# Attention scores from split queries and keys stacked to K = 128, heads taken group by group, and image 0's convolution inputs made in other steps

## The chip, the cores and the metric

The kernel runs on one core of one Trainium2 chip. The metric is the device time of one execution in microseconds (us), the median of the runs shown. Engines are named as in the profile: PE (TensorE matmuls), PEld (its weight loads), DVE (VectorE), ACT (ScalarE), POOL (GpSimd), SP (SyncE, which here issues DMAs).

## The reference

x has four images of 256 channels and 48 x 48 pixels (N = 2304 tokens). Two layers follow each other, both with a residual. Cut to what matters:

```python
def layer0(v):                                   # v = group_norm(x)
    h = relu(bn(conv3x3(v)))                     # 256 -> 256
    q, k, v = split(qkv_w @ h + qkv_b)           # 8 heads of d = 32
    attn = softmax(q.T @ k * d**-0.5)            # 2304 x 2304 per head
    return proj_w @ (v @ attn.T) + proj_b
def layer1(v):                                   # v = group_norm(x)
    g = conv3x3(v)                               # 45 logits per pixel
    outs = [v]
    for i, d in enumerate((1, 6, 12, 24, 36)):
        w = softmax(g[:, 9*i:9*i+9])             # over 9 taps
        outs.append(sum(shift(v, tap_k, d) * w[k] for k in range(9)))
    return batch_norm(conv1x1(concat(outs)))     # over all four images
x = x + layer0(group_norm(x))
x = x + layer1(group_norm(x))
```

## The kernel before

All arithmetic is fp32, but for one f32r matmul in the filters. Channels lie on the 128 partitions in two halves (NH = 2, index g); each half holds four heads of 32 channels. The program is written out in full, image after image, and each engine runs its instructions strictly in that written order; so do the DMAs that SP issues. Tiles come from pools with a fixed number of buffers, and an instruction that needs a buffer waits until its last user is done. DMAs of one queue take eight semaphores in turn, so a DMA also waits for the landing of the one eight before it.

Image 0 first runs its convolution and its q, k and v products alone. Then, for each image b, come two stages: attention of image b, and the dynamic filters of image b. Into the filter stage of image b the convolution and the q, k, v products of image b + 1 are woven, paced by how much DVE work a filter tap has. The last image's filter stage stands alone (`alone`), and after it the batch norm is applied and the output stored.

**Convolution** (`conv`, `inputs`, `outputs`, class `Made`). The 3 x 3 convolution is done in a transformed domain along rows: six positions, taken in the order `ORDER = (1, 2, 3, 4, 0, 5)`, each with its own transformed weights u and transformed input rows `v[i]`, for two halves of the rows. The input rows are made in three steps (`inputs(stage, g)`), by ACT's multiplications and, in image 0, DVE's additions; a table `when` says before which position each step is written. In image 0 the weights are made as well (`Made.pair`, `Made.__call__`), and stored to DRAM for the other images (`taken` reads them back). The results pass through a ring of two PSUM banks (`psum_tile` from `psc`); ACT copies positions 1 and 3 to tiles of tag `m1` (four buffers), DVE combines the others.

**q, k and v** (`conv_qkv`). For each of six chunks of 384 tokens, each half g and each of q and k, PE makes one product (two 128-row matmuls), ACT adds the bias and writes it to an SBUF tile that holds the whole image, and DVE takes the largest absolute value of it for a safety bound. Then the v products follow.

**Attention** (`attention`). A unit is 512 queries of one half g; 2304 is four times 512 and 256 over, so each image has eight units, two per stretch of 512 queries (both halves), and a ninth that holds the last 256 queries of both halves side by side. Each unit has 18 steps, one for every 128 keys. A step m has these parts, and the step's `weigh` is written after the next step's `scores`:

- `scores` (L891): for each of the four heads a matmul with K = 32, on the head's own 32 partitions, to two PSUM tiles of two banks each (three such tiles exist); then two ACT exps (L900) of 128 x 1024 to `p` (three buffers).
- `weigh` (L921): four matmuls with M = 32 that add v times p to `num`; and either DVE adds p to `acc` (L938), or, in steps 5 and 11, PE adds its column sums to `den` (L947).
- At the unit's end ACT copies `num` out (L943). Two steps into the next unit, `close` adds the column sums of `acc` to `den`, and DVE transposes, inverts and multiplies (L956 to L964).

Every fp32 matmul is two instructions in the trace, two passes. While units run, `project` (L996, L1005) makes the output projection of finished chunks, and twelve ACT instructions (L1528) normalise the next image. Before attention, SP is given the reloads of the image rows (`load_pad`, L1507) and the first weights of the next convolution.

**Dynamic filters** (`dynamic_filters`). For each tap PE spreads one row of filter weights over the partitions (L1239, an f32r matmul in one pass), DVE multiplies it with the shifted image (L1256, L1263), POOL adds it up (L1276), and PE mixes the result into the output (L1185). `pump` decides from `rate` how many of the waiting PE parts (mixes, the next logits, the next image's convolution) are written after each tap. Finished chunks are stored by SP (L1207).

Of the kernel before, what the change touches and what calls it, by code (L numbers as in the profile page):

```python
# [8 lines left out]
F32 = mybir.dt.float32  # L9
# [8 lines left out]
P = 128  # L18
# [27 lines left out]
def conv_preact_kernel(  # L46
# [479 lines left out]

    with tc.tile_pool(name="w", bufs=1) as wpool, tc.tile_pool(
# [21 lines left out]
        zeros = wpool.tile([P, D], F32, tag="zeros", name="zeros")  # L549
        nc.gpsimd.memset(zeros, 0.0)  # L550

        pick = wpool.tile([P, NG], F32R, tag="pick", name="pick")


        e1 = wpool.tile([P, 2 * TPC, 2, 64], F32, tag="e1", name="e1")
        nc.gpsimd.memset(e1, 0.0)
# [8 lines left out]

        lg = wpool.tile([P, CH], F32, tag="lg", name="lg")
        nc.gpsimd.memset(lg, 0.0)
# [25 lines left out]
        class Norm:  # L593


            def __init__(self, tag, b):
                self.name = f"{tag}_{b}"
                self.st = small.tile([P, NH, NCK, 6], F32, tag=f"st{tag}", name=f"st{self.name}")
                self.mv = small.tile([P, NH, 2], F32, tag=f"mv{tag}", name=f"mv{self.name}")
# [56 lines left out]
        class Made:  # L656
# [23 lines left out]
            def __call__(self, i):  # L680
                w, u = self.w, self.u
                if i == 3:
                    self.pair(3, range(NH), self.other)
# [11 lines left out]
        def conv(b, gn, psum_tile, weights, ready, pool, hid):  # L695
# [55 lines left out]
            def outputs(i, g, o, m):  # L751
# [15 lines left out]
                if i in (1, 3):  # L767
                    first[at] = pool.tile([P, TN], F32, tag="m1", name=f"m_{b}_{i}_{at}", bufs=4)
# [17 lines left out]
            if b == 0:  # L786
                when = {(0, 0): [(0, 0), (0, 1)], (1, 0): [(1, 0), (1, 1)], (3, 0): [(2, 0), (2, 1)]}
            else:
                when = {
                    (0, 0): [(0, 0), (0, 1), (1, 0), (1, 1)], (0, 1): [(2, 0), (2, 1)]  # L790
                }
            ahead = ready
            for at, i in enumerate(ORDER):
                u = ahead
                for g in range(2):
                    for stage, gg in when.get((at, g), ()):
                        inputs(stage, gg)
# [19 lines left out]
        def conv_qkv(b, gn, psum_tile, weights, ready, pool):  # L817

            hid = keep("h", f"hid_{b}")
            yield from conv(b, gn, psum_tile, weights, ready, pool, hid)  # L820
            q, k_ = keep("q", f"q_{b}"), keep("k", f"k_{b}")
            vT = act.tile([P, NT, C], F32, tag="v", name=f"vT_{b}")
            qkv[b] = q, k_, vT

            part = small.tile([P, 2, NH, NCK], F32, tag="qkpart", name=f"qkpart_{b}")
            top = small.tile([P, 2, NH], F32, tag="qktop", name=f"qktop_{b}")
            for c in range(NCK):
                cols = slice(c * CH, (c + 1) * CH)
                for g in range(NH):
                    for s, dst, bias in ((0, q, Q_B), (1, k_, K_B)):  # L830
                        pq = psum_tile(f"pq_{b}_{c}_{g}_{s}")
                        for i in range(NH):
# [6 lines left out]
                            )  # L839
                        nc.scalar.activation(  # L840
                            dst[:, g, cols], pq[:, :CH], AF.Identity, bias=vec[:, bias, g : g + 1]
                        )
                        nc.vector.tensor_reduce(
                            part[:, s, g, c : c + 1], dst[:, g, cols], AX.X, ALU.max,
                            apply_absolute_value=True,
                        )
                        yield 2 * MM
            for t in range(0, NT, 2):
# [23 lines left out]
        def attention(b, q, k_, vT, pools, spare, project):  # L872
# [3 lines left out]
            ao = keep("h", f"ao_{b}")  # L876

            whole, rest = N // QC * QC, N % QC
            units = [[(g, q0, QC, 0)] for q0 in range(0, whole, QC) for g in range(NH)]
            units.append([(g, whole, rest, g * rest) for g in range(NH)])  # L880
            assert NH * rest == QC
            heads = [slice(j * D, (j + 1) * D) for j in range(4)]

# [3 lines left out]
            def scores(u, m):  # L887
                ss = [ps2(f"se_{b}_{u}_{m}_{pair}") for pair in range(2)]
                for g, q0, n, at in units[u]:
                    for j, r in enumerate(heads):  # L890
                        nc.tensor.matmul(  # L891
                            ss[j // 2][:, j % 2, at : at + n],
                            k_[r, g, m * P : (m + 1) * P],
                            q[r, g, q0 : q0 + n],
                            start=True,
                            stop=True,
                        )
                p = work0.tile([P, 4, QC], F32, tag="p", name=f"p_{b}_{u}_{m}", bufs=3)
# [8 lines left out]
            def weigh(u, m, p):  # L907
                if m == 0:
# [5 lines left out]
                several = len(units[u]) > 1  # L914
                if several and m == 0:

                    for j, r in enumerate(heads):
                        nc.tensor.matmul(st["num"][r, :], zeros, p[:, j, :], start=True, stop=False)
                for i, (g, q0, n, at) in enumerate(units[u]):
                    for j, r in enumerate(heads):  # L920
                        nc.tensor.matmul(  # L921
                            st["num"][r, at : at + n],
                            vT[:, m, g * P + j * D : g * P + (j + 1) * D],
                            p[:, j, at : at + n],
                            start=(m == 0 and not several),
                            stop=(m == NT - 1 and i == len(units[u]) - 1),
                        )
                end = u == len(units) - 1
                direct = (DIRECT[0], NT - 1) if end else DIRECT
                if m in direct:  # L930
                    if m == DIRECT[0]:
                        st["den"] = ps_a.tile([P, 512], F32, tag="den", name=f"den_{b}_{u}")
                    sums(u, p, m == DIRECT[0], False)
                elif m == 0:
                    st["first"] = p
                else:
                    other = st["first"] if m == 1 else st["acc"]
                    nc.vector.tensor_tensor(st["acc"], other, p, ALU.add)  # L938
                if end:
                    st["out"] = st["num"]  # L940
                elif m == NT - 1:
                    st["out"] = work0.tile([P, QC], F32, tag="out", name=f"no_{b}_{u}")
                    nc.scalar.copy(st["out"], st["num"])  # L943

            def sums(u, rhs, start, stop):
                for j, r in enumerate(heads):
                    nc.tensor.matmul(  # L947
                        state[u]["den"][r, :], ones, rhs[:, j, :], start=start, stop=stop
                    )

            def close(u):

                sums(u, state[u]["acc"], False, True)
                st = state.pop(u)
                t = work0.tile([P, QC], F32, tag="rden", name=f"rt_{b}_{u}", bufs=1)
                nc.vector.transpose(t, st["den"])  # L956
                rc = work0.tile([P, QC // D], F32, tag="rc", name=f"rc_{b}_{u}")
                nc.vector.reciprocal(rc, t.rearrange("p (k d) -> p k d", d=D)[:, :, 0])
                nc.vector.transpose(
                    t.rearrange("p (k d) -> p k d", d=D),  # L960
                    rc.unsqueeze(2).to_broadcast([P, QC // D, D]),
                )
                for g, q0, n, at in units[u]:
                    nc.vector.tensor_tensor(  # L964
                        ao[:, g, q0 : q0 + n], st["out"][:, at : at + n], t[:, at : at + n],
                        ALU.mult,
                    )

            steps = [(u, m) for u in range(len(units)) for m in range(NT)]
            prev = None  # L970
            chunk = 0
            for i, (u, m) in enumerate(steps):
                ps = scores(u, m)
                if prev is not None:
                    weigh(*steps[i - 1], prev)
                prev = ps
                if m == 2 and u:
                    close(u - 1)
                if m == 6 and u % NH == 0:
                    while (chunk + 1) * CH <= units[u][0][1]:  # L980
                        project(chunk, ao, ps2(f"pp_{b}_{chunk}"))
                        chunk += 1
                if m > 2 and u > 1 and spare:
# [50 lines left out]
        def dynamic_filters(b, ao, chunk, norm, other, pools):  # L1034
# [89 lines left out]
            alone = b == B - 1  # L1124
# [494 lines left out]
```

## Time and profile before

| what | value |
|---|---|
| median of 3 runs | 3092.05 us (3091.05 to 3093.03) |
| profiled execution, its own time | 3093.91 us |
| its span | 3092.1 us |
| PE busy | 2875.9 us (93%) |
| DVE busy | 2354.6 us (76%) |
| ACT busy | 1547.9 us (50%) |
| POOL busy | 1108.2 us (36%) |
| scores and exps, image 0 | 155.4 to 548.3 us |
| scores and exps, image 1 | 889.8 to 1286.2 us |
| scores and exps, image 2 | 1627.9 to 2024.4 us |
| scores and exps, image 3 | 2364.0 to 2756.4 us |
| filter taps (L1263), image 0 | 593.7 to 880.6 us |
| filter taps (L1263), image 3 | 2800.6 to 3048.6 us |

Busy time is the time in which an engine had at least one instruction running, and matmul ends are modelled, so PE's share says less than the starts of its instructions. In a group's row, "x" is the number of instructions, then come busy time and the mean of one in ns, then the engine's idle time before them and what ended it.

### The profile page before, as it was taken

How to read it: one execution, taken by the hardware profiler on the slowest of the kernel's cores; microseconds unless marked ns; L12 is line 12 of the kernel's file. 1: busy time of each engine (PE TensorE's matmuls, PEld its weight loads, DVE VectorE, ACT ScalarE, POOL GpSimd, SP SyncE). 2: the span in 40 equal slices, each digit the busy share in tenths (PEclk: the TensorE clock that was granted, in tenths of full speed). 3: DMA queues.
4: the chain of work that ended last, by engine and by line, in shares of the span. 5: the costliest groups of instructions: out<-in, count | busy, mean ns of one | idle time of the engine just before them, and what ended most of it. 6: DMA issues, size and time to landing. Idle time of an engine off the chain costs nothing. (4 is left out here: it accounts for less than half of the span.)

```text
span 3092.1 us, 43492 instructions
## 1 busy us (share of the span) xinstructions
PE 2875.9 (93%) x17782; PEld 1326.9 (43%) x17782; DVE 2354.6 (76%) x2280; ACT 1547.9 (50%) x1812; POOL 1108.2 (36%) x833
## 2 busy tenths in 40 slices
PE   6999999998999999998999999999899999988984
PEld 4722224465542222465662222356565222244663
DVE  5478888578768888767867888867776898876766
ACT  3388878201248887600217887830114888750003
POOL 0000000797940000388890000069794000006794
PEclk9999999999999999999999999999999999998997
DMA  4400000001040000010003000000001000022004
GB/s 160 104 1 6 6 11 7 26 32 35 16 82 6 1 6 11 22 35 31 29 6 77 6 6 11 6 27 26 21 6 42 6 1 6 11 73 102 1 1 174
DMA packets 77968, 95.57 MB, mean 31 GB/s; under 512 B 52144, under 2 KB 66752, under 8 KB 75968
## 3 DMA queue, kind: packets, MB, share of 16 engines
q1 hardware_dynamic: 76960, 87.31, 9.8%
q0 software_dynamic: 800, 5.41, 0.4%
q8 instruction: 141, 2.31, 0.3%
q14 instruction: 67, 0.55, 0.1%
HBM read 62.03 MB, written 30.67 MB: 30 GB/s over the span
## 5 line engine op out<-in xcount | busy, mean ns | idle before, releaser
L900 ACT ACTIVATE p<-se 128x1024 f32<-128x1024 f32 x1296 | 1258.4, 1025 | 281.3 <-PE se L891 235.8
L938 DVE TENSOR_TENSOR acc<-acc,p 128x2048 f32<-128x2048 f32 x504 | 1154.6, 2291 | 110.1 <-ACT p L900 71.0
L1276 POOL TENSOR_TENSOR cat<-cat,prod 128x752 f32<-128x752 f32 (+7 forms) x734 | 992.4, 1361 | 589.3 <-issue 442.9
L891 PE MATMUL se<-q,k 32*128 32x512 f32 (+1 forms) x5760 | 806.9, 593 | 10.5 <-ACT p L900 7.4
L1263 DVE TENSOR_TENSOR prod<-wb,pad 128x768 f32<-128x768 f32 (+7 forms) x768 | 550.7, 746 | 208.9 <-PE wb L1239 171.7
L921 PE MATMUL num<-p,vT 128*32 128x512 f32 (+1 forms) x5760 | 695.3, 562 | 9.6 <-ACT no L943 7.4
L891 PEld LDWEIGHTS se<-q,k 32*128 32x128 f32 x5760 | 294.3, 183 | 525.6 <-issue 422.5
L716 POOL TENSOR_TENSOR cv_q<-pad,cv_q 128x600 f32<-128x600 f32 x3 | 5.4, 1791 | 1350.0 <-ACT cv_q L714 1350.0
L1239 PE MATMUL wb<-w,pick 128*128 128x384 f32 (+3 forms) x888 | 425.2, 517 | 24.1 <-DVE prod L1263 22.3
L1185 PE MATMUL py<-cat,wsc 128*128 128x384 f32 x960 | 364.8, 508 | 33.4 <-POOL cat L1276 33.2
L921 PEld LDWEIGHTS num<-p,vT 128*32 128x32 f32 x5760 | 121.8, 108 | 488.5 <-issue 439.5
L1185 PEld LDWEIGHTS py<-cat,wsc 128*128 128x128 f32 x960 | 183.1, 197 | 135.2 <-POOL cat L1276 42.7
L1239 PEld LDWEIGHTS wb<-w,pick 128*128 128x128 f32 x888 | 166.9, 193 | 140.1 <-DVE prod L1263 45.5
L805 PE MATMUL pc<-cv_q,u 128*128 128x288 f32 x576 | 168.8, 425 | 7.1 <-DVE cv_q L718 7.1
L805 PE MATMUL pc<-cv_k,u 128*128 128x288 f32 x576 | 163.2, 414 | 9.3 <-DVE cs L772 6.5
L1061 PE MATMUL pg<-pad,wcat 128*45 128x384 f32 x864 | 153.3, 498 | 2.4 <-DVE pad L589 1.5
L1256 DVE TENSOR_TENSOR cat<-wb,pad 128x768 f32<-128x768 f32 x120 | 114.2, 952 | 46.4 <-PE wb L1239 46.1
L744 ACT ACTIVATE hid<-yt,bn_t_f,bn_s 128x288 f32<-128x288 f32 x64 | 39.4, 625 | 202.6 <-DVE yt L757 116.2
L833 PE MATMUL pq<-hid,wqkv 128*128 128x384 f32 x384 | 135.7, 486 | 0.0
L938 DVE TENSOR_TENSOR acc<-p,p 128x2048 f32<-128x2048 f32 x36 | 82.5, 2292 | 65.1 <-ACT p L900 65.1
L805 PEld LDWEIGHTS pc<-cv_q,u 128*128 128x128 f32 x576 | 111.5, 200 | 35.1 <-DVE cv_q L718 7.2
L805 PEld LDWEIGHTS pc<-cv_k,u 128*128 128x128 f32 x576 | 108.2, 193 | 37.4 <-DVE cs L772 6.9
(209 smaller groups left out, 1676.7 us busy)
## 6 DMA issues: line engine op xcount, KB each, us to landing
pad<-in_x SPq DMA_DIRECT2D x14, 1152.0 KB, 15.2
u<-u_d SPq DMA_DIRECT2D x18, 768.0 KB, 4.3
x_d<-pad SPq DMA_DIRECT2D x48, 192.0 KB, 2.5
xst<-in_x SPq DMA_DIRECT2D x36, 192.0 KB, 2.4
y_d<-y SPq DMA_DIRECT2D x18, 384.0 KB, 2.7
u_d<-u SPq DMA_DIRECT2D x6, 768.0 KB, 3.7
y<-y_d SPq DMA_DIRECT2D x2, 2304.0 KB, 14.0
x<-x_d SPq DMA_DIRECT2D x2, 2304.0 KB, 21.3
```

Source lines behind the costliest of these rows:

```text
L805: nc.tensor.matmul(m, u[:, h, kx, o * P : (o + 1) * P], halves[g][:, h, i, :, kx : kx + WW], start=(h == 0 and kx == 0), stop=(h == NH - 1 ...
L833: nc.tensor.matmul(pq[:, :CH], wqkv[:, i, s, g * P : (g + 1) * P], hid[:, i, cols], start=(i == 0), stop=(i == NH - 1),)
L891: nc.tensor.matmul(ss[j // 2][:, j % 2, at : at + n], k_[r, g, m * P : (m + 1) * P], q[r, g, q0 : q0 + n], start=True, stop=True,)
L900: nc.scalar.activation(p[:, 2 * pair : 2 * pair + 2, :], ss[pair], AF.Exp, scale=QS)
L921: nc.tensor.matmul(st["num"][r, at : at + n], vT[:, m, g * P + j * D : g * P + (j + 1) * D], p[:, j, at : at + n], start=(m == 0 and not s ...
L938: nc.vector.tensor_tensor(st["acc"], other, p, ALU.add)
L1061: nc.tensor.matmul(pg[64 * s : 64 * s + NG, :CH], wcat[:, i, k, :], window(gn, i, (c + s) * R, k // 3 - 1, k % 3 - 1), start=(i == 0 and k ...
L1185: nc.tensor.matmul(to, wsc[:, n * NH + i, o * P : (o + 1) * P], rhs(i), start=(n == 0 and i == 0), stop=(last and i == NH - 1),)
L1239: nc.tensor.matmul(pw[:, : nr * WW], pick[:, k : k + 1].to_broadcast([P, P]), w[:, l0 * WW : l1 * WW], start=True, stop=True,)
L1256: nc.vector.tensor_tensor(catv, wb, src, ALU.mult)
L1263: nc.vector.tensor_tensor(pv, wb, src, ALU.mult)
L1276: nc.gpsimd.tensor_tensor(dst, dst, pv, ALU.add)
```

## The change

It has three parts.

1. **Scores.** `conv_qkv` no longer keeps q and k whole in SBUF. ACT writes the biased product rounded to f32r (`head`), DVE writes what the rounding left (`tail`, a scalar_tensor_tensor that reads PSUM and `head`), and SP stores both to DRAM (`qk_d`). `stack` reads them back so that one head's operands fill 128 partitions: head, tail, head, tail of the keys, and head, head, tail, tail of the queries. A score block is then one f32r matmul with K = 128 per head. Keys of one half g lie in two tiles, reloaded for g = 1 as the last unit of g = 0 uses them up; queries are loaded a unit ahead by 16 DMAs per unit.
2. **Units.** They now run half by half: four units of 512 and one of 256 queries for g = 0, then for g = 1. A unit of 256 takes two blocks of keys per step, so nine steps. `close`'s and `num`'s work tiles are parts of one buffer of the pool of transformed weights; the row reloads and the next weights are issued after the first two units' queries (`begin`). The `zeros` matmuls go; `lg` and `e1` are made once per image.
3. **Image 0's convolution.** The second half of the rows is normalised after the first input step of the first half; the second input step of both halves and the weights for positions 3 and 4 are made before the second half of position 1; the third step comes one half position earlier. In the last filter stage `rate` loses its factor of 1.5.

```diff
+    qk_d = tc.dram_tile([2, 2, P, NH, N], F32, name="qk_d")
...
-                if i == 3:
-                    self.pair(3, range(NH), self.other)
...
             if b == 0:
-                when = {(0, 0): [(0, 0), (0, 1)], (1, 0): [(1, 0), (1, 1)], (3, 0): [(2, 0), (2, 1)]}
+                when = {
+                    (0, 0): [(0, 0), 0, (0, 1)], (0, 1): [(1, 0), (1, 1), 1],
+                    (2, 1): [(2, 0), (2, 1)],
+                }
...
+        def stack(dst, s, parts, g, j0, nj, cols):
+            for at, part in enumerate(parts):
+                nc.sync.dma_start(
+                    out=dst[at * D : (at + 1) * D].bitcast(F32),
+                    in_=qk_d[s, part, j0 * D : (j0 + nj) * D, g, cols].rearrange(
+                        "(j d) n -> d j n", d=D
+                    ),
+                )
+        def keys_of(keys, g, c):
+            cols = slice(c * CH, (c + 1) * CH)
+            for pair in range(2):
+                stack(keys[pair][:, :, cols], 1, (0, 1, 0, 1), g, 2 * pair, 2, cols)
...
-                        nc.scalar.activation(
-                            dst[:, g, cols], pq[:, :CH], AF.Identity, bias=vec[:, bias, g : g + 1]
+                        head, tail = (
+                            pool.tile([P, CH], F32, tag="m1", name=f"{n}_{b}_{c}_{g}_{s}", bufs=4)
+                            for n in ("head", "tail")
+                        )
+                        of = vec[:, bias, g : g + 1]
+                        nc.scalar.activation(
+                            head.bitcast(F32R), pq[:, :CH], AF.Identity, bias=of
+                        )
+                        nc.vector.scalar_tensor_tensor(
+                            out=tail.bitcast(F32R), in0=pq[:, :CH], scalar=of, in1=head,
+                            op0=ALU.add, op1=ALU.subtract,
                         )
...
+                        nc.sync.dma_start(out=qk_d[s, 0, :, g, cols], in_=head)
+                        nc.sync.dma_start(out=qk_d[s, 1, :, g, cols], in_=tail)
                         yield 2 * MM
+                if c:
+                    keys_of(keys, 0, c - 1)
+            keys_of(keys, 0, NCK - 1)
...
+            units = [(g, q0, min(QC, N - q0)) for g in range(NH) for q0 in range(0, N, QC)]
...
+            def queries(u, js):
+                g, q0, n = units[u]
+                for j in js:
+                    t = work0.tile([P, 1, QC], F32R, tag="qs", name=f"qs_{b}_{u}_{j}", bufs=8)
+                    stack(t[:, :, :n], 0, (0, 0, 1, 1), g, j, 1, slice(q0, q0 + n))
+                    qs[u, j] = t
...
-                for g, q0, n, at in units[u]:
-                    for j, r in enumerate(heads):
+                n = units[u][2]
+                for j in range(4):
+                    for m, cols in blocks(u, i):
                         nc.tensor.matmul(
-                            ss[j // 2][:, j % 2, at : at + n],
-                            k_[r, g, m * P : (m + 1) * P],
-                            q[r, g, q0 : q0 + n],
+                            ss[j // 2][:, j % 2, cols],
+                            keys[j // 2][:, j % 2, m * P : (m + 1) * P],
+                            qs[u, j][:, 0, :n],
                             start=True,
                             stop=True,
                         )
...
+            for u in range(2):
+                queries(u, range(4))
+            begin()
...
+                if i == 0 and 0 < u < len(units) - 1:
+                    queries(u + 1, range(4))
...
+                if u + 1 < len(units) and units[u + 1][0] != g:
+                    while (fetched + 1) * CH <= (blocks(u, i)[-1][0] + 1) * P:
+                        keys_of(keys, units[u + 1][0], fetched)
+                        fetched += 1
...
-            if alone:
-                mixes *= 1.5
...
+                        rows(0, HH // 2 + 2)
+                        weights.pair(ORDER[0], [1], weights.home)
+                        between = (
+                            lambda: rows(HH // 2 + 2, HH),
+                            lambda: weights.pair(3, range(NH), weights.other),
+                        )
```

## The prediction

> **What bounds the kernel now.** First the page's costliest groups, those of attention's scores.
>
> ```profile
> L900 ACT ACTIVATE p<-se 128x1024 f32<-128x1024 f32 x1296 | 1258.4, 1025 | 281.3 <-PE se L891 235.8
> ...
> L891 PE MATMUL se<-q,k 32*128 32x512 f32 (+1 forms) x5760 | 806.9, 593 | 10.5 <-ACT p L900 7.4
> ```
>
> The exp waits for the scores (235.8 us), the scores hardly for anything. Next the table of stretches: attention of image 0, the q and k products of image 0, and those of image 1, which lie inside the filter stage.
>
> ```profile
> 156.00:548.00 392.00, 388.33 (x3122) 118.36 (x3114) 335.86 (x191) 326.22 (x350) 0.00 (x0) 1.00 0.03 6
> 107.00:138.00 31.00, 31.00 (x98) 18.28 (x97) 15.49 (x29) 13.97 (x24) 0.00 (x0) 1.00 0.61 120
> 776.00:850.00 74.00, 69.52 (x241) 43.43 (x239) 57.41 (x92) 15.42 (x26) 69.64 (x54) 1.00 0.06 17
> ```
>
> Columns: length, then busy PE, PEld, DVE, ACT, POOL. PE leads in all three; DVE has 56 us free per image's attention, but 17 of 74 in the last row. Third, PE's timeline in attention:
>
> ```profile
> 982.94 1.14 PE L891 MATMUL se<-q,k 32*128 32x512 f32 x8
> 984.01 1.06 PE L921 MATMUL num<-p,vT 128*32 128x512 f32 x8
> 985.01 1.31 PE L891 MATMUL se<-q,k 32*128 32x512 f32 x8
> 986.25 1.06 PE L921 MATMUL num<-p,vT 128*32 128x512 f32 x8
> ...
> 994.06 2.85 PE L996 MATMUL pp<-ao,wp 128*128 128x384 f32 x8
> 996.84 1.14 PE L891 MATMUL se<-q,k 32*128 32x512 f32 x8
> ```
>
> Starts count here, since ends are modelled. A score block takes 1.07 us unhindered (982.94 to 984.01) and 1.24 when its second pair must wait for exp to free a PSUM pair; num takes 1.00. A plain step averages 2.155 (exp starts 2.13 and 2.18 apart), and a plain unit is 41.55 (L943, one copy per unit: 936.83, 978.37): 18 x 2.155 plus two direct sums of 0.88 and a closing one of 0.97. So PE's sum alone sets a unit.
>
> **Scores.** Before, four heads run at once in 32-row tiles, each in two fp32 passes. L996 shows the parts: 2.78 us for eight passes of 384 columns. Passes of L1185 start 0.322 apart, so 8 x 0.322 = 2.58 and 0.20 is left for the first weight load and the change of tiling. A 512-column pass is 0.427 and 2 x 0.427 + 0.20 = 1.05: the 1.07 is explained. The new matmul is f32r, one pass, K = 128, four in a row. Its price is in the q and k products, where a filter matmul (f32r, 384 columns) stands between fp32 passes:
>
> ```profile
> 843.10 1.45 PE L833 MATMUL pq<-hid,wqkv 128*128 128x384 f32 x4
> 844.10 0.63 PE L1239 MATMUL wb<-w,pick 128*128 128x384 f32 x1
> 844.57 1.45 PE L833 MATMUL pq<-hid,wqkv 128*128 128x384 f32 x4
> ```
>
> 1.47 - 4 x 0.322 = 0.18; start to start in the instruction records the least is 0.169. An fp32 column costs 0.84 ns, so half of that is 0.160 for 384: 0.009 is added per instruction. For 512 columns: 0.213 + 0.009 = 0.222. A new block is 0.20 + 4 x 0.222 = **1.09**; from below 0.20 + 4 x 0.213 = 1.05, from above 4 x 0.24 (0.18 scaled) + 0.20 = 1.16. One pass for four heads in a row is thus worth what two passes of four heads at once are worth; the gain is only that pairs now finish 0.45 us apart, so that the wait for exp (0.09 on average) goes. The step becomes 2.085, 0.07 less.
>
> The Trainium skill speaks against even that: "TensorE: Matmul & The Clock Gate", The mechanism, says that a weight load overlaps running matmuls only when the row group differs, and here all four use all rows. By it each block would show three more loads. The rows disagree: L1185's loads start 2 ns after the matmul before, and the next matmul starts 0.322 on, pure column time. The same page (Back-to-back issue gap) gives N / 2.4 + 2.5 ns, 216 ns for 512 columns: a block of 1.06, which would add 0.03 us to the gain per step.
>
> Per image: eight full units, 8 x 18 x 0.07 = -10.1. The shared last unit (41.72) becomes two half units of nine steps: each block is 8 matmuls of 256 columns (0.107 + 0.009, say 0.119; most of 192 columns took 0.110) + 0.20 = 1.15, so 18 x 2.15 + five sums 4.6 = 43.3, +1.6. In the 12 steps that also hold L1528's normalisation ACT is the bound (two exps issued 0.92 apart and 0.7, over 2.085) and nothing is gained: +0.8 in three images. Sum **-32 us** (-60 with 1.05, +8 with 1.16). DVE's add (2.396 start to start) is longer than a step and lags 0.31 per step; three p buffers leave some 1.8, and direct steps give 2 back, so I take no stall.
>
> **Start of attention.** Rows of the timeline at image 1:
>
> ```profile
> 889.74 0.51 SPq L1207 DMA_DIRECT2D y_d<-y  x1
> ...
> 889.76 1.99 PE L891 MATMUL se<-q,k 32*128 32x512 f32 x12 [0.93 <-ACT y L1203]
> ...
> 893.07 3.77 ACT L900 ACTIVATE p<-se 128x1024 f32<-128x1024 f32 x4 [3.36 <-DMA y_d<-y]
> ```
>
> Scores are ready today and exp starts when y's store lands. In the new order on SP the 16 loads of unit 0's queries stand behind that store, and the first waits for its landing too. SP issues 0.37 apart (72.32 to 72.69) to 0.50 (x_first: four in 2.02); I take 0.42, and 2.2 to land (1.9 and 2.4 for 192 KB). Head 3 is there at 893.1 + 6.7 + 2.2 = 902.0, its exp at 902.4 against 894.0: +8.4. After an idle PE the next 24 passes of the convolution took 8.23 for 5.98 (rows below); I add 1. Three images: **+28** (20 to 35). For image 0 the v products (15.7 us) cover the loads: +1. The pads' four loads (6 us each on SP) and u_1 move behind 32 query loads; they are needed some 100 us later (L1528 at 996), so free; unit 2's queries behind them still precede unit 2.
>
> **Split of q and k.** Each of 24 products per image gains a scalar_tensor_tensor on DVE (0.61 by L1005) and two stores, on four m1 buffers: two products in flight. A buffer pair turns in exp-like head 0.58 + DVE 0.61 + issue 0.42 + landing 2.4 + hand-overs 0.2 = 4.2 us, 2.1 per product, against 1.30 on PE (31.1 / 24). Each chunk of four also puts eight key loads (3.4 us) on SP ahead of the next stores, of which about 1.3 is not hidden: 9.7 per chunk. Image 0: 8.4 + 5 x 9.7 = 57 for 31, less 4 that the v products overlap: **+22** (from 93 issues x 0.37 = 34: +4, to +30). Images 1 to 3 spread the products 3.1 us apart, so the buffers turn in time, but DVE gains 14.7 us in the 74 us row with 17 free. PE and POOL lead there (94%), so I take a third: **+14** (0 to 44). If that cover is gone, it is the 44.
>
> **Image 0's convolution.**
>
> ```profile
> 48.20 8.23 PE L805 MATMUL pc<-cv_k,u 128*128 128x288 f32 x24 [6.49 <-DVE cs L772]
> ...
> 67.90 5.98 PE L805 MATMUL pc<-cv_q,u 128*128 128x288 f32 x24
> 76.10 4.14 PE L805 MATMUL pc<-cv_k,u 128*128 128x288 f32 x9 [2.22 <-DVE cs L775]
> ```
>
> The second-stage inputs and the pair for u_3 now run while the first products do, so DVE is free when the outputs come: 6.49 falls to 0.5, the slow passes (8.23 - 5.98) go, 2.22 goes, and half the rows' normalisation (0.82) leaves the start: **-11** (-12 to -8). In the last filter stage the factor 1.5 goes, and mixes lie one tap further apart: -2 (-6 to 4). Memsets of lg and e1 fall on an idle POOL; zeros goes: 0.
>
> Sum: -32 + 28 + 1 + 22 + 14 - 11 - 2 = **+20**. The profiled execution took 3093.91 (span 3092.1) and becomes 3114; the median, 3092.05, becomes **3112 us**.
>
> **Rivals.** *Free switch, faster:* between whole-array matmuls and the column tiles the first load and the drain (0.20) are hidden, so a block is 0.90. A unit would be 36.2, but DVE's 15 adds and closing (38.5) then bound it at 39.0: -2.6 x 9 = -92 in four images, 3052. For it: L996 to L891 shows 0.20 only at fp32. Against it: f32r matmuls are followed by L1061's column tiles 0.262 to 0.268 later, by L805's 0.171. It decides from a gain of 13 us per image on, a step under 2.065. *Exposed loads, slower:* each of four loads (0.107, as for transposes 0.108 apart) is seen: block 1.41, step 2.40, +0.25 x 162 x 4 = +162, 3294 with the other terms. L1185's rows are against it. *The split fills the filter stage:* DVE's 14.7 is paid whole and late stores hold DVE and ACT: +44 for +14, 3142. For it: 94% on PE and POOL at once.
>
> **Chances.** Forecast 0.62 (3075 to 3140); free switch 0.20; exposed loads 0.06; full filter stage 0.12. About 0.2%, 6 us, is what a measurement can tell from no change: between 3086 and 3098 I put 0.10 (0.09 of the forecast's, 0.01 of the free switch's), faster 0.25 (0.06 and 0.19), slower 0.65. The range 3060 to 3150 reaches into the free switch below and past the full stage above.
>
> **What would show it.** Right: score blocks of 1.05 to 1.16, plain units near 40.3, first exps some 8 us after y lands, q and k products of image 0 over some 55 us with head waiting for DMA, no 6.49 gap. Wrong: blocks under 1.0 or over 1.3; head 3's queries landed before y; products still 31 us long.

## The result, and the profile after

The changed kernel took 3119.03 us (median of 4 runs, 3116.03 to 3121.70) beside 3091.55 us of the kernel before on the same chip: a ratio of 1.0091, 95% interval 1.0074 to 1.0109, some 28 us slower. The forecast was 3112. The profiled execution took 3118.67 us, its span 3116.9, which is 24.8 more than the span before.

First the costliest groups of the page, the two lines that answer to those of before:

```profile
L958 ACT ACTIVATE p<-se 128x1024 f32<-128x1024 f32 x1296 | 1261.7, 1031 | 277.2 <-PE se L949 218.7
...
L949 PE MATMUL se<-qs,keys_q 128*128 128x512 f32 (+1 forms) x1440 | 481.3, 423 | 25.1 <-DMA qs<-qk_d 24.8
```

exp waits 17 us less for the scores than before (218.7 for 235.8), but the scores now wait 24.8 us for queries, a wait that did not exist. Next the table of stretches (length, then busy PE, PEld, DVE, ACT, POOL, clock, DMA share, GB/s): the q and k products of image 0, and those of image 1 inside the filter stage.

```profile
97.20:144.80 47.60, 37.98 (x97) 18.18 (x95) 26.28 (x50) 13.41 (x23) 0.00 (x0) 0.93 0.76 245
779.70:861.80 82.10, 73.64 (x239) 43.36 (x238) 68.26 (x115) 15.52 (x26) 69.55 (x54) 0.98 0.50 164
```

They took 31 and 74 us before. In the second, PE, ACT and POOL do the same work as before within some 4 us; only DVE has more to do, 68.26 for 57.41. PE's timeline in attention:

```profile
1001.51 0.73 PE L949 MATMUL se<-qs,keys_q 128*128 128x512 f32 x2
1002.09 0.63 PE L949 MATMUL se<-qs,keys_k 128*128 128x512 f32 x2
1002.64 1.07 PE L976 MATMUL num<-p,vT 128*32 128x512 f32 x8
1003.64 0.73 PE L949 MATMUL se<-qs,keys_q 128*128 128x512 f32 x2
```

A block of scores takes 1.13 us here (1001.51 to 1002.64; over the steps that stand between two num the median is 1.125, most lie from 1.115 to 1.131), num 1.00, a plain unit 40.7. The start of attention in image 1:

```profile
901.10 0.52 SPq L1281 DMA_DIRECT2D y_d<-y  x1
...
903.97 12.39 SPq L822 DMA_DIRECT2D qs<-qk_d  x27
...
907.47 0.76 PE L949 MATMUL se<-qs,keys_q 128*128 128x512 f32 x1 [7.23 <-DMA qs<-qk_d]
...
910.05 1.02 ACT L958 ACTIVATE p<-se 128x1024 f32<-128x1024 f32 x1 [8.98 <-DMA qs<-qk_d]
...
912.87 0.76 PE L949 MATMUL se<-qs,keys_k 128*128 128x512 f32 x1 [1.16 <-DMA qs<-qk_d]
```

SP issues the first query load when y's store has landed, 2.9 us after its issue, and then one every 0.46 us; one head's scores follow another 1.6 to 1.9 us apart. The fourth head's scores start 11.8 us after y's copy ended (901.07), and the first num 14.2 after it; before, that was 5.5.

| where (us) | before | after | difference |
|---|---|---|---|
| image 0: start to end of the convolution | 107.2 | 97.4 | -9.8 |
| image 0: end of the convolution to first exp | 49.4 | 70.5 | +21.1 |
| first to last exp, images 0 to 3 | 391.7, 393.1, 393.3, 389.2 | 384.9, 389.9, 389.7, 384.4 | -18.4 |
| last exp to the next image's first, three times | 344.8, 344.9, 342.8 | 357.2, 358.0, 354.0 | +36.7 |
| image 3's last exp to the end | 335.7 | 330.9 | -4.8 |

### The profile page after: what moved, and what is told of

It is laid out like the page before. It is cut to its first block, busy times and chain, and to the rows that moved or that the text cites. A ratio compares the mean times of both kernels' runs of the same rounds, so it can differ in the third digit from the quotient of the medians.

```text
span 3116.9 us, 40446 instructions
## 1 busy us (share of the span) xinstructions
PE 2867.5 (92%) x15094; PEld 1504.1 (48%) x15094; DVE 2385.4 (77%) x2380; ACT 1549.0 (50%) x1816; POOL 1111.0 (36%) x838
## 5 line engine op out<-in xcount | busy, mean ns | idle before, releaser
L958 ACT ACTIVATE p<-se 128x1024 f32<-128x1024 f32 x1296 | 1261.7, 1031 | 277.2 <-PE se L949 218.7
L991 DVE TENSOR_TENSOR acc<-acc,p 128x2048 f32<-128x2048 f32 x492 | 1127.1, 2291 | 106.7 <-ACT p L958 67.2
L949 PE MATMUL se<-qs,keys_q 128*128 128x512 f32 (+1 forms) x1440 | 481.3, 423 | 25.1 <-DMA qs<-qk_d 24.8
L949 PEld LDWEIGHTS se<-qs,keys_q 128*128 128x128 f32 x1440 | 213.9, 189 | 529.7 <-issue 512.1
L1313 PE MATMUL wb<-w,pick 128*128 128x384 f32 (+3 forms) x888 | 434.8, 523 | 30.7 <-DVE prod L1337 29.6
L949 PE MATMUL se<-qs,keys_k 128*128 128x512 f32 (+1 forms) x1440 | 411.7, 375 | 9.5 <-DMA qs<-qk_d 7.2
L949 PEld LDWEIGHTS se<-qs,keys_k 128*128 128x128 f32 x1440 | 255.0, 189 | 68.0 <-ACT p L958 10.3
L804 PE MATMUL pc<-cv_q,u 128*128 128x288 f32 x576 | 172.4, 432 | 12.5 <-POOL cv_q L709 6.2
L853 PE MATMUL pq<-hid,wqkv 128*128 128x384 f32 x384 | 146.5, 510 | 19.9 <-DVE tail L869 18.9
L866 ACT ACTIVATE head<-pq,vec 128x384 fp32r<-128x384 f32 x96 | 55.8, 581 | 206.3 <-PE pq L853 163.9
L991 DVE TENSOR_TENSOR acc<-p,p 128x2048 f32<-128x2048 f32 x40 | 91.7, 2293 | 83.5 <-ACT p L958 49.4
## 6 DMA issues: line engine op xcount, KB each, us to landing
pad<-in_x SPq DMA_DIRECT2D x14, 1152.0 KB, 14.7
```

The lines of the kernel that those rows point to most:

```text
L804: nc.tensor.matmul(m, u[:, h, kx, o * P : (o + 1) * P], halves[g][:, h, i, :, kx : kx + WW], start=(h == 0 and kx == 0), stop=(h == NH - 1 ...
L853: nc.tensor.matmul(pq[:, :CH], wqkv[:, i, s, g * P : (g + 1) * P], hid[:, i, cols], start=(i == 0), stop=(i == NH - 1),)
L949: nc.tensor.matmul(ss[j // 2][:, j % 2, cols], keys[j // 2][:, j % 2, m * P : (m + 1) * P], qs[u, j][:, 0, :n], start=True, stop=True,)
L958: nc.scalar.activation(p[:, 2 * pair : 2 * pair + 2, :], ss[pair], AF.Exp, scale=QS)
L1313: nc.tensor.matmul(pw[:, : nr * WW], pick[:, k : k + 1].to_broadcast([P, P]), w[:, l0 * WW : l1 * WW], start=True, stop=True,)
```

## The experiments

The theory was the prediction's: the scores' form gains, and the feeding of it (query loads behind y's store, the split's DVE work, its buffers and SP's issue) costs more. Each run undoes or does one part. Differences below are those of the ratios to the kernel before, in parts of 3088 us; the changed kernel stands at 1.0091, and a difference between two ratios is uncertain by some 6 us.

**The convolution's order alone**, on the kernel before:

```diff
-when = {(0, 0): [(0, 0), (0, 1)], (1, 0): [(1, 0), (1, 1)], (3, 0): [(2, 0), (2, 1)]}
+when = {(0, 0): [(0, 0), 0, (0, 1)], (0, 1): [(1, 0), (1, 1), 1], (2, 1): [(2, 0), (2, 1)]}
...
```

Expected: 

> The kernel before with image 0's convolution inputs in the new order and nothing else of the change. Theory: the two waits for DVE of 6.49 and 2.22 us go and the stage from 21.1 to 107.2 us becomes some 9.7 us shorter, as it did in the changed kernel; nothing behind it gives that back, so the time is 3092 - 10 = 3082 us (3079 to 3084). Rival: the stage's end is not what the time rests on, because the q and k products behind it wait for something of their own (a DMA, DVE); then 5 us or less are gained, 3087 or more.

Measured: 0.9972 (0.9961 to 0.9982), 8.6 us faster. In its trace the q and k products behind still take 31.1 us and everything later is as before. The gain is real and nothing gives it back.

**And without the factor of 1.5:**

```diff
-            if alone:
-                mixes *= 1.5
```

Expected: 

> As the run with image 0's order alone, and also without the factor of 1.5 on the mixes in the last filter stage. Theory of the prediction: the factor is worth 2 us (a loss of 4 to a gain of 6), so 3080 us, and the stretch of the last stage's taps becomes 248.0 - 3 = 245 us long, as in the changed kernel. Rival: the 2.9 us by which the changed kernel's last stage is shorter come from its smaller last unit of attention; then this run stands at the 3082 us of the other and the stretch stays 248 us.

Measured: 0.9977 (0.9968 to 0.9986), no different from the run without it. The stretch of the last stage's taps did fall, from 247.9 to 244.9 us, so the factor is worth the 3 us in the trace that the changed kernel shows there; a whole run's time does not resolve it.

**The old form of the scores in the new kernel:**

```diff
-                for j in range(4):
-                    for m, cols in blocks(u, i):
+                for m, cols in blocks(u, i):
+                    for j in range(4):
...
-                            keys[j // 2][:, j % 2, m * P : (m + 1) * P],
-                            qs[u, j][:, 0, :n],
+                            keys[j // 2][heads[j], j % 2, m * P : (m + 1) * P].bitcast(F32),
+                            qs[u, j][heads[j], 0, :n].bitcast(F32),
```

Expected: 

> The changed kernel (its split, its DMAs, its units) with the scores' matmuls in the old form: 32 rows, fp32 in two passes, four heads in four row groups at once, on the 32 rows of the stacked tiles that lie at their head's place, so that the scores hold one of the four partial products. Theory of the prediction: only the form of the matmuls is worth the gain in attention (1.26 us per plain unit forecast, 0.85 seen), so plain units go back to 41.55 us and the time is 27 to 40 us above the changed kernel's: 3146 to 3160 us. Rival: the gain in the units comes from their order and smaller closings, not from the matmuls' form; then plain units stay at 40.7 and the time within 6 us of 3119.

Measured: 1.0220 (1.0206 to 1.0234), 40 us above the changed kernel. Plain units are 41.58 us again (40.69 in the changed kernel), the half unit 21.39 (20.92). In image 0, whose start is not held up, first to last exp is 393.1 us: 1.4 more than in the kernel before, the price of the new units and their order, and 8.2 more than in the changed kernel, the gain of the form. The rival (the units' order makes the gain) falls.

**One DMA instead of four for a head's queries.** The two parts are stored next to each other, so that 64 rows, repeated, fill the 128; the stores of the queries then go to four groups of 32 rows, and the keys are stacked as head, head, tail, tail:

```diff
-                    stack(t[:, :, :n], 0, (0, 0, 1, 1), g, j, 1, slice(q0, q0 + n))
+                    nc.sync.dma_start(
+                        out=t[:, 0, :n].bitcast(F32),
+                        in_=q_d[j, :, :, g, q0 : q0 + n].rearrange("a d n -> (a d) n")
+                        .unsqueeze(0).to_broadcast([2, 2 * D, n]),
+                    )
...
```

Expected: 

> The changed kernel with the queries' two parts stored so that one DMA (a repeated source, 128 rows) brings a head's stacked queries instead of four. Theory of the prediction: the start of attention in images 1 to 3 is set by 16 issues on SP of 0.46 us each after y's store has landed, and then the landing; with 4 issues head 3 is there 12 x 0.46 = 5.5 us earlier, so the first num comes some 5.5 us earlier in three images, 16 us in all, and image 0 gains about 1: 3119 - 17 = 3102 us (3099 to 3106). Rival: the transfers, not their issue, set the start (the same bytes by 128 rows in one DMA land later, or are queued behind y's store); then head 3 lands within 2 us of before the edit and 6 us or less are gained, 3113 or more.

Measured: 1.0646 (1.0628 to 1.0664), 171 us slower than the changed kernel. Neither theory expected that. SP's timeline in image 0's attention, and the stretch of the same time, whole and from 200 to 220, when the last key loads are through:

```profile
191.50 31.10 SPq L928 DMA_DIRECT2D qs<-q_d  x8
```

```profile
191.00:222.00 31.00, 17.48 (x75) 11.28 (x73) 2.61 (x3) 8.07 (x11) 0.00 (x0) 0.72 0.16 55
200.00:220.00 20.00, 6.74 (x20) 2.75 (x19) 0.83 (x2) 3.88 (x4) 0.00 (x0) 0.58 0.13 50
```

Eight loads held SP for 31.1 us, 3.9 each, while the DMA engines were 0.13 busy: two of sixteen. The stores into four groups of 32 rows were slow too: image 0's products took 76.9 us, those of images 1 to 3 95 to 96, and DVE's tails waited for them (46.0 us in image 0). The edit shows that fewer issues are no gain where the transfers themselves get slow, and says nothing of the start's cause.

**Half the first queries on ACT's queue:**

```diff
...
+                          nc.scalar if u == 0 and j > 1 else None)
```

Expected: 

> The changed kernel with the queries of heads 2 and 3 of each image's first unit issued on ACT's queue, beside SP's for heads 0 and 1. Theory of the prediction: SP's issue of 0.46 us each sets the start of attention, so head 3 lands 8 x 0.46 = 3.7 us earlier in images 1 to 3: 3119 - 11 = 3108 us (3106 to 3112). Rival: the transfers or ACT's own order set it (two queues share what lands, ACT's issues hold up its first exp); then 4 us or less are gained, 3115 or more.

Measured: 1.0091 (1.0076 to 1.0107), no gain. First the loads on ACT's queue in image 0, then the start of image 1:

```profile
166.20 3.67 ACTq L822 DMA_DIRECT2D qs<-qk_d  x8
...
911.05 12.05 SPq L822 DMA_DIRECT2D qs<-qk_d  x24
911.08 6.56 ACTq L822 DMA_DIRECT2D qs<-qk_d  x8
...
918.18 1.02 ACT L959 ACTIVATE p<-se 128x1024 f32<-128x1024 f32 x1 [10.03 <-DMA qs<-qk_d]
```

In image 1 ACT's loads started 0.82 us apart in the mean for SP's 0.50 beside them. ACT itself issues no slower: one issue took 0.31 to 0.45 us there, and in image 0 the eight came 0.46 apart. But both queues draw on the same eight semaphores, and in images 1 to 3 each of ACT's loads from the third on started 0.02 to 0.06 us after a load of SP's had landed, the one that had used its semaphore last. Head 3's scores started 11.5, 10.8 and 11.9 us after y's copy for 11.8, 12.1 and 12.5, and the first exp, which stands behind the issues on ACT, came 10.03, 9.60 and 10.74 after it for 8.98, 9.41 and 8.96. Still the first unit was 2.3 to 2.7 us shorter, so that images 1 to 3 gained 1.6, 2.4 and 0.5 us up to their second unit. Image 0 lost them again: there ACT issued its loads only after its last copy of v, and the first unit took 44.4 us for 39.3. The rival's time holds, by ACT's own order and the shared semaphores; the run says little of SP's issue.

**The first queries where no store of y is waited for** (heads 0 to 2 in a u buffer):

```diff
+                    if u == 0 and j < 3:
+                        t = spot[:, j * QC : (j + 1) * QC].unsqueeze(1)
+                    else:
+                        t = work0.tile([P, 1, QC], F32R, tag="qs", ...)
...
```

Expected: 

> The changed kernel with the queries of heads 0 to 2 of each first unit in one of the two u buffers, whose memory is free, so that they wait for no store of y (head 3 stays where it was; u_1's load moves behind unit 2's queries). Theory of the prediction: the first of the 16 loads waits for the landing of y's last store, 2.9 us in the trace; without it head 3 lands some 2.5 us earlier in three images: 3119 - 8 = 3111 us (3109 to 3114). Rival: it costs nothing, because exp itself waits for that landing; then 3117 to 3121.

Measured: 1.0081 (1.0066 to 1.0097), 3 us for 8 expected, which a run's time does not tell from nothing. In the trace the first num comes 12.3, 12.5 and 12.3 us after y's copy for 14.2, 14.5 and 14.9: the wait for y's landing is worth about 2.2 each, as thought; two of its filter stages (the taps' stretches) were 2.5 and 2.9 us longer in that execution, which stays unexplained.

**The first queries loaded ahead of time.** The half unit comes first; its queries fit the free u buffer and are issued during the v products:

```diff
+            units.insert(0, units.pop(N // QC))
...
+            first_qs = [spot[:, j * rest : (j + 1) * rest].unsqueeze(1) for j in range(4)]
+            for j, t in enumerate(first_qs):
+                stack(t, 0, (0, 0, 1, 1), 0, j, 1, slice(N - rest, N))
...
```

Expected: 

> The changed kernel with head group 0's half unit as the first unit, whose 16 query loads (256 columns, 4 KB per partition in all) go into a free u buffer during the v products, ahead of y's last store; unit 1's queries go where unit 0's went. Theory of the prediction: all that the start of attention costs in images 1 to 3 (the first num 14.2 us after y's copy against 5.5 before) is query loads behind y's store, so the first num comes at 5.5 to 6.5 us and 3 x 8 = 24 us are gained: 3119 - 24 = 3095 us (3091 to 3100). Rival: the start is given back, since unit 1's queries, issued as late as unit 0's were, hold unit 1 after only 21 us, or 16 more issues and loads in the filter stage hold that up; then less than 8 us are gained, 3111 or more.

Measured: 1.0007 (0.9998 to 1.0016), 26 us faster than the changed kernel, and level with the one before.

```profile
898.59 0.52 SPq L1289 DMA_DIRECT2D y_d<-y  x1
...
898.62 0.74 PE L956 MATMUL se<-spot,keys_q 128*128 128x256 f32 x4 [0.89 <-ACT y L1285]
...
901.50 3.77 ACT L965 ACTIVATE p<-se 128x1024 f32<-128x1024 f32 x4 [2.94 <-DMA y_d<-y]
```

Scores stand ready, and exp waits for y's landing alone, as in the kernel before. The first num comes 5.0, 4.9 and 7.2 us after y's copy. Unit 1, whose queries are issued as late as unit 0's were, waits for nothing (the first unit takes 20.8 us and its neighbour 40.7). The cause of the start's price is shown.

**The split without DVE:**

```diff
-                        nc.vector.scalar_tensor_tensor(
-                            out=tail.bitcast(F32R), in0=pq[:, :CH], scalar=of, in1=head,
-                            op0=ALU.add, op1=ALU.subtract,
-                        )
...
-                        nc.sync.dma_start(out=qk_d[s, 1, :, g, cols], in_=tail)
+                        nc.sync.dma_start(out=qk_d[s, 1, :, g, cols], in_=head)
```

Expected: 

> The changed kernel without the 96 scalar_tensor_tensor of the split: the head is stored a second time in the tail's place, so that all buffers, stores and loads stay and the scores lose the low part. Theory (the prediction's, with a larger size): in images 1 to 3 the q and k products take 82.1, 82.1 and 78.9 us in the filter stage instead of 74 because DVE carries 14.7 us more; without it they go back to 74 to 76, 18 us in three images; image 0's chain of buffers gets 0.6 shorter per turn, some 6 us: 3119 - 24 = 3095 us (3090 to 3102). Rival: the stores, their landing and SP's issue hold the four buffers, not DVE; then the products stay over 80 us and the time above 3110.

Measured: 1.0007 (0.9998 to 1.0016), 26 us faster than the changed kernel, for 24 expected.

```profile
774.50:848.50 74.00, 69.91 (x239) 43.35 (x238) 57.63 (x93) 15.50 (x26) 69.62 (x54) 1.00 0.57 182
```

The products of images 1 to 3 take 73.9 us each, as before the change (there 75.4 in image 2), with DMA share 0.57 where it was 0.06. So all stores and key loads of the split are free in the filter stage, and the whole 20 us there are DVE's 14.7 us per image. Image 0's products fall only from 47.6 to 43.3.

**Tail on SBUF instead of PSUM:**

```diff
-                        nc.vector.scalar_tensor_tensor(
...
+                        nc.scalar.activation(tail, pq[:, :CH], AF.Identity, bias=of)
+                        nc.vector.tensor_tensor(tail.bitcast(F32R), tail, head, ALU.subtract)
```

Expected: 

> The changed kernel with the tail's first operand written to SBUF by ACT (bias added) and a tensor_tensor on SBUF in place of DVE's scalar_tensor_tensor on PSUM. Theory: DVE's length is what the filter stage pays (14.7 us more of DVE cost it 8 us per image); by the adds' 1.12 ns per column the new DVE instruction takes 0.45 to 0.5 for 0.61, 2.6 to 3.8 us per image less on DVE, so the stretches of the products get some 2 us shorter: 3119 - 6 = 3113 us (3109 to 3117). Rival: ACT's extra 0.58 us per product lengthens the chain in which buffers turn and nothing is gained: 3118 to 3130.

Measured: 1.0184 (1.0170 to 1.0198), 29 us slower. The groups of DVE in image 1's products, this run's line and then the changed kernel's:

```profile
L870 DVE TENSOR_TENSOR tail<-tail,head 128x384 fp32r<-128x384 f32 x23 | 21.6, 940 | 10.4 <-ACT tail L869 10.3
```

```profile
L869 DVE SCALAR_TENSOR_TENSOR tail<-pq,vec,head 128x384 fp32r<-128x384 f32 x23 | 14.0, 610 | 8.6 <-ACT head L866 8.6
```

The instruction got longer, not shorter: 0.94 us in the mean, up to 2.11, where in image 0, with POOL idle, it took 0.56. The products grew to 92.8, 91.4 and 87.7 us. ACT's wait is part of it too, so the run does not divide the loss; that DVE's length is what the stage pays fits again, with the other sign.

**Twelve buffers in image 0, and its key loads on POOL's queue:**

```diff
...
+pool.tile([P, CH], F32, tag="m1", ..., bufs=4 if b else 12)
...
```

The copies of image 0's convolution share the tag and have twelve buffers too.

Expected: 

> The changed kernel with 12 instead of 4 buffers for heads and tails in image 0 alone. Theory of the prediction: the turn of four buffers through ACT, DVE, store and landing sets image 0's products (47.6 us and a gap of 3.3 ahead of v, for 31.1 us before); with 12 they take 33 to 40 and the first exp comes 8 to 15 us earlier: 3119 - 11 = 3108 us (3103 to 3112). Rival: SP's issue sets them (96 stores and key loads of 0.42 us, 40 us, and the queries behind them, 7 us more); then the first exp comes 4 us earlier at most, 3115 or more.

Measured: 1.0085 (1.0069 to 1.0101), 2 us. The products take 39.1 us for 47.6 and the first exp comes 9.8 us earlier, as the theory said; but it stands 6.4 us behind v's end, not 2.5, and the second pair's exp follows 5.05 us later, not 0.92. The query loads, 14.2 us of issue, now start at 152.0, when v has ended: the cover that the prediction named for image 0 is gone. Then the second edit:

```diff
...
+keys_of(keys, 0, c - 1, None if b else nc.gpsimd)
...
```

Expected: 

> As the run with 12 buffers in image 0, and the 48 key loads of image 0 issued on POOL's queue, where POOL has nothing to do, instead of SP's. Theory: SP's issue was what remained there (heads and tails waited for SP behind key loads, the last key load was issued 0.3 us after v's end and the queries behind it), so the products take 32 to 36 us for 39.1, the first exp comes 2 to 4 us after v for 6.4, and the time is 3116 - 10 = 3106 us (3102 to 3110). Rival: POOL issues so much slower (ACT took 0.82 us each for SP's 0.46) that the keys come late and hold the first unit; then 3114 or more.

Measured: 1.0046 (1.0032 to 1.0059), 14 us faster than the changed kernel. The first exp comes 2.5 us after v and the next 0.92 later. POOL issued in 0.53 us each; its loads landed in 4.4 to 4.8 us for SP's 2.3, which here is early enough. So SP's issue held the attention of image 0. The products, against the theory, stay at 39.2:

```profile
96.20:135.40 39.20, 34.51 (x98) 16.37 (x96) 26.77 (x52) 13.99 (x25) 19.69 (x37) 1.00 0.93 313
```

The DMA engines are 0.93 busy. PE's rows divide the 8.1 us above the 31.1 of before:

```profile
96.16 14.59 PE L853 MATMUL pq<-hid,wqkv 128*128 128x384 f32 x40
112.71 8.86 PE L853 MATMUL pq<-hid,wqkv 128*128 128x384 f32 x24 [1.96 <-DVE tail L869]
123.67 11.64 PE L853 MATMUL pq<-hid,wqkv 128*128 128x384 f32 x32 [2.10 <-DVE tail L869]
```

The two stops, 4.1 us, are DVE standing 2 us for a block of the next image's x, with tails behind it. The other 4 us are passes some 0.365 apart for 0.324 before: DVE's tail now reads each product from PSUM after ACT, and PE's weight loads wait for tails 15.0 us in all. No run took these apart, or told them from the load on the DMA engines.

**Three edits together** (half unit first with its queries ahead, 12 buffers, POOL's queue):

Expected: 

> The changed kernel with three edits at once: the half unit first with its queries loaded ahead, 12 buffers in image 0, and image 0's key loads on POOL's queue. Theory: the gains lie in different places (the starts of images 1 to 3; image 0's products) and add up, -26 and -14, so 3119 - 40 = 3079 us (3075 to 3085), below the kernel before by some 10 us; what is left of the change's price is then DVE's part of the split, 20 us, and the scores' gain of 31 us is seen at last. Rival: in image 0 both use the same slack on SP and ahead of v's end, so that part of it counts once; then 3086 or more, no more than the kernel before.

Measured: 3074.99 us, 0.9954 (0.9941 to 0.9968): 42 us faster than the changed kernel for 40 expected, and 14 us (10 to 18) faster than the kernel before. The gains add up. It is the fastest version of this study. But 8.6 of the 14 us are the convolution's order, which alone stands at 0.9972 (0.9961 to 0.9982): what the scores' new form and the dropped factor leave when these repairs are made, some 6 us, is no more than the uncertainty of such a difference.

## Why the prediction was right, step by step

Slower, by the forecast's own mechanism; the sum was +20 us for 24.8 in the trace. Two of the sum's large terms came out close by errors that cancel, and that part is luck.

- **Scores, -32 forecast, about -29 found, by errors that cancel.** The -29 is the table's -18.4 less the 10.6 by which the first unit of images 1 to 3 is held up at its start (44.1 to 44.8 us there, 39.3 in image 0; before, 41.9 and 40.4). The step that was mis-sized is the matmul's price. 0.222 us for 512 columns was scaled from 384-column filter matmuls; the instruction records show 0.229 to 0.237, so the block is 1.125, not 1.09, and a plain unit 40.69: 0.86 gained, not 1.26, or 27.5 us in four images for 40.3. The normalisation adds 6.05 to a plain unit (46.74 - 40.69) where it added 4.03 before (48.35 - 44.32, both with a projection): +6 in three images for +2.4. What makes up for both is the last unit, +6.4 forecast and -4.8 found. The shared unit's 41.72 is a length that the rows show for the eighth unit of image 3; the shared one takes 44.4 from its first exp to its last, with a projection, and the two half units 20.92 and 22.27. The rest lies mostly in the projections (2.57 for 2.77 us each). The rivals of the free switch (block 0.90) and of exposed loads (1.41; its time, by the terms of the sum, would have been 3306 and not 3294) are both out by the 1.125. With it the rule weighed in the prediction, that weight loads overlap only between row groups (the Trainium skill, "TensorE: Matmul & The Clock Gate", The mechanism), does not show here.
- **Start, +28 forecast, 27.5 found** (16.9 before the first exp and 10.6 behind it), and shown by the run with the queries ahead. The wait for y's landing is about a quarter of it; the rest is SP's issue and the loads' landing, which no run took apart.
- **Split in image 0, +22 forecast, 21 found, by another route than told.** The products were to take 57 us, 4 of them under v; they took 47.6, but v started 3.3 later and took 17.3 for 15.7. Four buffers were to make all of it; with twelve, 8.5 of the 16.5 us on the products go. Without DVE's instruction, on four buffers, 4.3 go.
- **Split in the filter stage, +14 forecast, 20 found.** Of the sum's terms this one was furthest off. "A third of 14.7" should have been nearly a half: 8.2, 6.7 and 5.0 us. DVE was 57 of 74 busy, but its products feed POOL one by one, and one that stands behind a tail comes late to an engine that is 94% busy. POOL's adds in image 1's products show it, before, in the changed kernel and in the run without DVE's part:

```profile
L1276 POOL TENSOR_TENSOR cat<-cat,prod 128x576 f32<-128x576 f32 (+7 forms) x54 | 71.8, 1340 | 4.4 <-DVE prod L1263 1.4
```

```profile
L1350 POOL TENSOR_TENSOR cat<-cat,prod 128x576 f32<-128x576 f32 (+7 forms) x54 | 71.9, 1341 | 12.6 <-DVE prod L1337 9.7
```

```profile
L1346 POOL TENSOR_TENSOR cat<-cat,prod 128x576 f32<-128x576 f32 (+7 forms) x54 | 71.8, 1341 | 4.4 <-DVE prod L1333 1.4
```

POOL's busy time stays, and its idle time grows by 8.2 us, as the stretch does. That DVE's work and no DMA is to blame is shown by the run without it.
- **Convolution, -11 forecast, -9.8 in the trace and -8.6 in the run alone.** The waits of 6.49 and 2.22 went, but a new one of 2.40 for ACT's copy came, and 24 slow passes with it (7.78 us) that were to go:

```profile
31.40 7.78 PE L804 MATMUL pc<-cv_k,u 128*128 128x288 f32 x24 [2.40 <-ACT m L761]
```

- **Last filter stage, -2 forecast, -4.8 behind the last exp**, of which the taps are 2.9, in the trace; not resolved in time.

## What to carry to other kernels

Price a faster form of a matmul together with what feeds it: here the form gained 29 us, and the queries' late loads (27.5), an engine's extra 15 us per image (20) and the first image's buffers and issues (21) took some 69. Slack counts only where the new work falls, so read it from the waits of the stage's bound engines and not from a share of idle time. The loads of a stage's first operands should be issued ahead of the last store of the stage before it, and a smaller first unit can make them fit into memory that is already free.

## What the runs showed of the hardware

- A load of 256 KB whose source is two repeats of 64 rows took 3.9 us on SP with 0.13 of the DMA engines busy; four loads of 64 KB and 32 rows took 0.46 each and landed in 1.9. The Trainium skill, "DMA: Bandwidth & Descriptors", Why a DMA increments its semaphore by 16 and not by 1, says that a DMA runs on the largest number of engines up to 16 that divides both sides' slowest dimension. For two repeats that is two engines of sixteen, and the 0.13 agrees.
- A DVE subtraction of two SBUF operands took 0.56 us with POOL idle and 0.94 in the mean (0.54 to 2.11) beside POOL's adds, while the form that reads PSUM took 0.61 in both. The Trainium skill, "GPSIMD Engine Reference", Specifications, names contention with DVE instructions that have two SBUF inputs; the numbers agree.
- DMAs were issued 0.46 to 0.50 us apart on SP, 0.46 on ACT in image 0 and 0.53 on POOL, with median landings of 1.9 to 2.3, 2.5 and 4.4 to 4.8 us.
- Two queues that draw on the same semaphores hold each other up: on ACT's queue beside SP's, six of eight loads waited until a load of SP's that had used their semaphore had landed, and the eight took 6.56 us where in image 0 they took 3.67.
